# A list-scheduled attention and recurrence kernel: new latencies in its planner, another chunking of the recurrence, another layout of the output

## The chip, the cores and the metric

The kernel runs on one core of a Trainium2 chip. Its time is the device time of one launch in microseconds (us). The engines are called as in the profile: PE (matmul), ACT (activations), DVE (vector), POOL (GpSimd), and SP, which only issues DMAs.

## The reference

`x` holds 8 batches of 1024 tokens of 128 channels, all fp32. Cut to what matters:

```
# layer 0, per batch; 8 heads; a token is a pair (m of 64, g of 16)
scores = q @ k.T / sqrt(128)
a = softmax(softmax(scores over m) over g)
z1 = LN(a @ v @ wo.T + bo + x);  x = LN(relu(z1 @ w1.T + b1) @ w2.T + b2 + z1)
# layer 1, per batch
B = LN(x);  Wi = B @ W.T
scores[i, j] = sum_d v[d] * tanh(Wi[i, d] + Wi[j, d])
t = x + softmax(scores over j) @ B
# layer 1, recurrence over the 1024 tokens, 8 batches side by side
Wx = batch_norm(LN(t) @ W.T);  y[n] = sigmoid(Wx[n] + y[n-1] @ V.T);  out = t + y
```

The scores of layer 1 are symmetric, so some half million pairs per batch, each with 128 tanh, have to be computed.

## The kernel before, in words

`fast_path` does the work; `general_path` is a second program that runs only if a comparison of the inputs' sizes, made at the start, comes out as 0.

**The planner.** The main part is not written in the order in which it runs. Every piece of work is given to a `Plan` (L409) with its engine or a choice of engines, a weight in us for each, what it reads and writes, a priority (lower goes first) and, where it needs one, a choice of buffers. `Plan.emit` (L455) is a list scheduler. It goes through planned time; among the operations that can start within 0.15 us of the earliest start it takes the one of lowest priority number, and writes it at the end of its engine's instruction queue. An operation counts as ready when each producer is done, plus a latency that depends on the producer's engine: `LATENCY` (L425) if the producer ran on another engine, `AGAIN` (L426) if on the same one. The planned times appear nowhere in the program: only the order that they led to, and the choice of engine and of buffer. On the chip each engine takes its queue in that order, and waits by semaphores.

**Layer 0** (`layer0`, L784). For each head and each pair of query tiles: scores on PE (L851) into one of two PSUM tiles `sc`, an exponential on ACT (L854), sums, reciprocals and a division on DVE (L858, L859, L862), a second exponential for the pair on ACT (L871), sums and reciprocals on DVE (L874, L875), a division on POOL (L885), eight transposes on PE (L765) that DVE copies out into `aT` (L777), the product with the values on PE (L899), and an addition on DVE (L906). Small products and transposes go through two PSUM banks, m0 and m1 (`through_bank`). Of the first batch DVE or ACT may empty the banks.

**Layer 1's attention** (`layer1`, L1090, and `group`, L971). The tanh of a row tile are made in groups of k rows by 4. The planner chooses one of three ways for each group when its first row is placed: ACT adds and takes the tanh row by row (L994); or DVE (L998, one operation for each row, which also writes an accumulator) or POOL (L1004, one operation for k rows) adds, and ACT then takes one wide tanh over the group (L1040). Five buffers `th` hold groups. PE multiplies by v (L1057), four groups of 32 columns side by side. After all rows of a tile come an exponential (L1153), products with `B` (L1186) and the addition to X (L1191), whose result t is stored to DRAM in `parked` (L1205) and, normed and projected, to `parked_wx`. While ACT and PE do batch b's attention, batch b + 1's layer 0 runs beside it.

**The recurrence** (from L1324). The 1024 steps are cut into 64 chunks of 16 tokens that run side by side. All chunks are run twice: 16 steps from zero, which give each chunk the state that its neighbour ends with, and then 16 that are kept. (The state forgets fast enough; the comparison at the start tests what this needs.) A step is done in two halves of 32 chunks by 8 batches, 256 columns: `ident` times `ws` (L1365) and V times the previous `y` (L1367) add up in PSUM, ACT takes the sigmoid (L1369), and in the second round DVE copies `y` into `ys` (L1374). `ws` is the normed input in the order of the steps, made by 16 DVE operations (L1346).

**The output.** For each half of the tokens and each batch, PE transposes four tiles (L1382) into one of two PSUM banks, DVE adds `xr`, which is t read back from `parked` (L1340), into one of three buffers `ot` (L1384), and a DMA stores 256 KB (L1386), issued in turn by ACT and SP. A partition of `ot` holds four tokens that lie 128 apart, so the pieces in DRAM are 512 bytes.

Of the kernel before, what the change touches and what calls it, by code (L numbers as in the profile page):

```python
# [9 lines left out]
F32 = mybir.dt.float32  # L10
AF = mybir.ActivationFunctionType
ALU = mybir.AluOpType
AX = mybir.AxisListType
PSUM = bass.MemoryType.PSUM

P = 128
# [382 lines left out]
class Bank:  # L399


    def __init__(self, *choice):
        self.choice = choice

    def __call__(self):
        return self.tile
# [2 lines left out]
class Plan:  # L409
# [12 lines left out]

    LATENCY = {"PE": 0.12, "ACT": 0.08, "DVE": 0.08, "POOL": 0.15, "SP": 8.0}  # L425
    AGAIN = {"PE": 0.0, "ACT": 0.0, "DVE": 0.04, "POOL": 0.1, "SP": 8.0}  # L426

    def __init__(self):
        self.ops = []
# [25 lines left out]
    def emit(self, slack=0.15, switch=0.1, stay=0.015):  # L455
        ops, by = self.ops, self.by
        after = [[] for _ in ops]
        left = []
        for n, o in enumerate(ops):
            before = o[4] | set(o[7])  # L460
            left.append(len(before))
            for d in before:
                after[d].append(n)
        engines = list(self.LATENCY)
        open_ = {e: [] for e in engines}
        free = dict.fromkeys(engines, 0.0)
        done = [0.0] * len(ops)
        began = [0.0] * len(ops)
        places = [None] * len(ops)
        mode = "full"  # L470
        bank_free = {}
        port_free = 0.0
        never = float("inf")
        self.order = []

        def ready_at(n, e):
            t = max((began[d] for d in ops[n][7]), default=0.0)
            for d in ops[n][4]:
                t = max(t, done[d] + (self.AGAIN if by[d] == e else self.LATENCY).get(by[d], 0.0))
            return t  # L480

        def start_at(n, t, e):
            take = ops[n][5]
            if take:
                t = max(t, min(bank_free.get(c[0], 0.0) for c in take.choice))
            if e == "POOL" or (e == "DVE" and ops[n][8]):
                t = max(t, port_free)
            return max(t, free[e])

        def release(n):  # L490
            where = ops[n][0]
            where = where() if callable(where) else where
            if where is None:
                began[n] = done[n] = ready_at(n, None)
                finish(n)
                return
            places[n] = {p[0]: (*p[1:], 0.0) for p in (where if isinstance(where, list) else [where])}
            for e in places[n]:
                open_[e].append((n, ready_at(n, e)))

        def finish(n):
            for a in after[n]:
                left[a] -= 1
                if left[a] == 0:
                    release(a)

        for n in [n for n, c in enumerate(left) if c == 0]:
            release(n)
        while any(open_.values()):
            first, e = min(  # L510
                (min(start_at(n, t, e) for n, t in open_[e]), i) for i, e in enumerate(engines) if open_[e]
            )
            assert first < never
            e = engines[e]
            n, start = min(
                ((n, s) for n, s in ((n, start_at(n, t, e)) for n, t in open_[e]) if s <= first + slack),
                key=lambda c: (ops[c[0]][2][0] + places[c[0]][e][1] + (stay if e == "PE" and ops[c[0]][3] != mode else 0), c[0]),
            )
            _, fn, _, m, _, take, give, _, port = ops[n]
            if take:  # L520
                take.name, take.tile = min(take.choice, key=lambda c: bank_free.get(c[0], 0.0))
                bank_free[take.name] = never
            cost = places[n][e][0]
            if e == "PE":
                if m != mode:
                    cost += switch
                mode = m
            free[e] = start + (cost if e != "SP" else 0.2)
            if e == "POOL" or (e == "DVE" and port):
                port_free = start + cost  # L530
            began[n], done[n], by[n] = start, start + cost, e
            for q in places[n]:
                open_[q] = [c for c in open_[q] if c[0] != n]
            if give:
                bank_free[give.name] = done[n] + self.LATENCY[e]
            self.order.append((n, e, start, done[n]))
            fn(e)
            finish(n)
# [22 lines left out]
def fast_path(ctx: ExitStack, tc: tile.TileContext, a: dict, fits):  # L561
# [5 lines left out]
    nc = tc.nc  # L567
    NB, N, C = a["x"].shape
    H = a["wqn"].shape[1]
    NT = N // P  # L570
# [1 line left out]
    G = 16  # L572
    M = N // G
    SCALE = 1.0 / math.sqrt(C)
    NCH = 64
    LCH = N // NCH
    NX = 2
    NE = 2
# [3 lines left out]
    dram = ctx.enter_context(tc.tile_pool(name="dram", bufs=1, space=bass.MemoryType.DRAM))  # L582
# [4 lines left out]
    def tile_of(pool, name, shape):  # L587
        return pool.tile(shape, F32, tag=name, name=name)
# [6 lines left out]
    wx = tile_of(keep, "wx", [P, NB, N])  # L595
    parked_wx = [tile_of(dram, f"parked_wx{b}", [P, N]) for b in range(NB - 1)]
    wx_stats = tile_of(keep, "wx_stats", [P, NB, 2, 6])

    parked = [tile_of(dram, f"parked{b}", [P, NT, C]) for b in range(NB)]

    def load(pool, name, shape, eng):
        t = pool.tile(shape, F32, tag=name, name=name + "_sb")
# [50 lines left out]
    vf_sb = load(const, "vf", [P, C], nc.sync)  # L653
# [8 lines left out]
    ident = tile_of(const, "ident", [P, P])  # L662
# [308 lines left out]
    def group(it, at0, r0, k, wiT, all_wi, L1, ROWS, fillers, chain, left, both, first_half):  # L971
# [6 lines left out]
        w = N - i0  # L978
# [17 lines left out]
        def add_row(c, r):  # L996

            nc.vector.tensor_scalar(  # L998
                rows(c)[:, r, :], wiT[:, i0 + begin[c] :], w_i(c, r), 0.0, ALU.add, ALU.add, accum_out=unused
            )  # L1000

        def add_rows(eng, c):
# [10 lines left out]
            "POOL": [  # L1013
                (0.27 + 1.62e-3 * k * (w - begin[c]), lambda c=c: add_rows(nc.gpsimd, c)) for c in range(4)
            ],
            "DVE": [(0.30 + 1.04e-3 * (w - begin[c]), lambda c=c, r=r: add_row(c, r)) for c, r in each]
            if k < 4
            else [(0.15 + 1.04e-3 * k * (w - begin[c]), lambda c=c: add_rows(nc.vector, c)) for c in range(4)],
        }
# [152 lines left out]
    def attention(b, it, X, kX, B, kB, E_at, L1):  # L1172
# [27 lines left out]
        if it % 4 != 3:  # L1200
# [1 line left out]
        qh = it // 4  # L1202
        Xg = X[:, 4 * qh : 4 * qh + 4, :]
        add(
            ("SP", 4.0), lambda _: nc.sync.dma_start(out=parked[b][:, 4 * qh : 4 * qh + 4, :], in_=Xg),  # L1205
            r=[kg], w=[("parked", b, qh)], pri=L1,
        )
        layer_norm(Xg, kg, B2, kB2, 4, L1)
# [125 lines left out]
    nc.vector.tensor_tensor(off, beta_sb, off, ALU.subtract)  # L1334


    ys = rn.tile([P, NB, N], F32, tag="ys", name="ys")
    xr = rn.tile([P, NB, NT, C], F32, tag="xr", name="xr")
    for b in range(NB):
        nc.sync.dma_start(out=xr[:, b], in_=parked[b])  # L1340
    steps = ys.rearrange("p b (c l) -> p c b l", l=LCH)

    ws = rn.tile([P, LCH, NCH, NB], F32, tag="ws", name="ws")
    for l in range(LCH):
        step = wx.rearrange("p b (c l) -> p l c b", l=LCH)[:, l]
        nc.vector.tensor_scalar(ws[:, l], step, sc, off, ALU.mult, ALU.add)  # L1346

    with tc.tile_pool(name="ps_w", bufs=2, space=PSUM) as ps_w, tc.tile_pool(
        name="ps_t", bufs=2, space=PSUM
    ) as ps_t:
        HC = NCH // 2
        prev = [None, None]
        for k in range(2 * LCH):
            l = k % LCH
            early = k < LCH
            for half in range(2):
                c0, c1 = half * HC, (half + 1) * HC  # L1360
                skip = 1 if early and half == 0 else 0
                src = ws[:, l, c0 + skip - early : c1 - early, :]
                acc = ps_w.tile([P, HC, NB], F32, tag=f"acc{half}", name=f"acc{half}")
                to = acc[:, skip:, :]
                nc.tensor.matmul(to, ident, src, start=True, stop=k == 0)  # L1365
                if k:
                    nc.tensor.matmul(to, vf_sb, prev[half][:, skip:, :], start=False, stop=True)  # L1367
                y = rn.tile([P, HC, NB], F32, tag=f"y{half}", name=f"y{half}", bufs=3)
                nc.scalar.activation(y[:, skip:, :], to, AF.Sigmoid)  # L1369
                if k == LCH - 1 and half == 0:  # L1370

                    nc.vector.memset(y[:, 0:1, :], 0.0)
                if not early:
                    nc.vector.tensor_copy(steps[:, c0:c1, :, l], y)  # L1374
                prev[half] = y

        n = 0
        for g in range(NT // 4):
            for b in range(NB):
                pt = ps_t.tile([P, 4, C], F32, tag="yt", name="yt")  # L1380
                for i in range(4):
                    nc.tensor.transpose(pt[:, i, :], ys[:, b, (4 * g + i) * P : (4 * g + i + 1) * P], ident)  # L1382
                ot = rn.tile([P, 4, C], F32, tag="ot", name="ot", bufs=3)
                nc.vector.tensor_tensor(ot, pt, xr[:, b, 4 * g : 4 * g + 4, :], ALU.add)  # L1384
                eng = nc.sync if n % 2 else nc.scalar
                eng.dma_start(  # L1386
                    out=a["out"][b, 4 * g * P : 4 * (g + 1) * P, :].rearrange("(t p) c -> p t c", p=P), in_=ot
                )
                n += 1

# [66 lines left out]
```

## Time and profile before

| what | value |
|---|---|
| three timed runs | 5790.97, 5794.7, 5795.5 us; median 5794.7 |
| the profiled execution's own time | 5790.2 us |
| its span, first to last instruction | 5788.3 us |
| mean granted TensorE clock | 0.970 |
| largest groups on POOL, PE and ACT | L1004 3167.8 us, L1057 2121.8 us, L994 2231.2 us, L1040 2069.4 us |
| main part, about | 0 to 5708 us |
| recurrence | 5709.5 to 5766.6 us |
| output | 5765.8 us to the end |

A line of the profile's groups names the line, the engine, what is written from what, the form and the number of times; then the busy time, the mean of one, and the idle time of the engine just before. A line of the waits names who waited for whom; then us in total, times and the longest. A line of the timeline begins with its start and its duration in us, and ends with the idle time before it and what ended that. A row of the stretches gives the length of the stretch and, for PE, PEld (weight loads), DVE, ACT and POOL, the busy time and the number of instructions.

### The profile page before, as it was taken

How to read it: one execution, taken by the hardware profiler on the slowest of the kernel's cores; microseconds unless marked ns; L12 is line 12 of the kernel's file. 1: busy time of each engine (PE TensorE's matmuls, PEld its weight loads, DVE VectorE, ACT ScalarE, POOL GpSimd, SP SyncE). 2: the span in 40 equal slices, each digit the busy share in tenths (PEclk: the TensorE clock that was granted, in tenths of full speed). 3: DMA queues.
4: the chain of work that ended last, by engine and by line, in shares of the span. 5: the costliest groups of instructions: out<-in, count | busy, mean ns of one | idle time of the engine just before them, and what ended most of it. 6: DMA issues, size and time to landing. Idle time of an engine off the chain costs nothing.

```text
span 5788.3 us, 97417 instructions
## 1 busy us (share of the span) xinstructions
PE 5221.0 (90%) x38885; PEld 2783.0 (48%) x38885; DVE 4697.6 (81%) x7236; ACT 5282.6 (91%) x4978; POOL 4218.7 (73%) x2714
## 2 busy tenths in 40 slices
PE   8899999999889999899998998899998999986567
PEld 6555544555445455454554554444554454443125
DVE  7899766877897788977998788977889678898885
ACT  5489999999999999999998999999998999999993
POOL 2352798788788879798786887788796887863871
PEclk9999999999999999999999999999998999998998
DMA  2000000000000000000000000000000000000001
GB/s 59 1 4 1 1 1 5 7 3 1 1 5 8 1 1 5 5 5 1 1 5 5 5 1 1 5 8 1 1 1 3 6 1 1 1 26 8 1 1 63
DMA packets 27328, 37.79 MB, mean 7 GB/s; under 512 B 2464, under 2 KB 19232, under 8 KB 26864
## 3 DMA queue, kind: packets, MB, share of 16 engines
q1 hardware_dynamic: 21760, 27.99, 1.5%
q8 instruction: 307, 5.03, 0.4%
q10 hardware_dynamic: 4944, 3.16, 0.2%
q14 instruction: 157, 1.29, 0.1%
q0 software_dynamic: 160, 0.33, 0.0%
HBM read 19.41 MB, written 12.06 MB: 5 GB/s over the span
## 4 chain that ended last, share of the span: by engine, by line
PE 52%; DVE 23%; ACT 19%; issue 4%; POOL 2%; DMA 0%; DVEq 0%; ACTq 0%; POOLq 0%; SPq 0%
PE sa L1057 19%; PE m L899 11%; PE sc L851 9%; ACT th L1040 8%; ACT th L994 7%; PE m L765 6%; DVE aT L777 2%; DVE th L1004 2%; DVE th L998 2%; DVE stat_e L874 2%; DVE stat_e L858 2%; ACT wx L871 2%; ACT sc L854 2%; DVE wx L862 2%; DVE X L737 2%
## 5 line engine op out<-in xcount | busy, mean ns | idle before, releaser
L1004 POOL TENSOR_TENSOR th<-wiT 128x1024 f32<-128x1024 f32 (+52 forms) x2124 | 3167.8, 1526 | 405.9 <-PE sa L1057 337.5
L1057 PE MATMUL sa<-th,vpat 128*32 128x512 f32 (+33 forms) x24576 | 2121.8, 470 | 230.9 <-ACT th L1040 219.4
L994 ACT ACTIVATE th<-wiT 128x128 f32<-128x128 f32 (+60 forms) x3092 | 2231.2, 795 | 13.7 <-PE sa L1057 13.5
L1040 ACT ACTIVATE th<-th 128x2490 f32<-128x2490 f32 (+50 forms) x760 | 2069.4, 2745 | 98.9 <-DVE th L998 52.5
L885 POOL TENSOR_TENSOR wx<-wx,stat_e 128x1024 f32<-128x1024 f32 x512 | 992.5, 1959 | 862.2 <-DVE stat_e L875 600.9
L1057 PEld LDWEIGHTS sa<-th,vpat 128*32 128x32 f32 x24576 | 674.8, 112 | 1480.7 <-issue 854.4
L851 PE MATMUL sc<-xT,wx 128*128 128x512 f32 x2048 | 982.2, 604 | 24.8 <-DVE wx L862 23.4
L899 PE MATMUL m<-aT,wx 128*128 128x256 f32 x3584 | 883.1, 394 | 15.1 <-DVE aT L777 13.6
L899 PEld LDWEIGHTS m<-aT,wx 128*128 128x128 f32 x3584 | 668.6, 194 | 269.0 <-issue 112.8
L998 DVE TENSOR_SCALAR_CACHE_REDUCE th<-wiT 128x328 f32<-128x328 f32 (+36 forms) x960 | 681.0, 709 | 83.9 <-PE sa L1057 17.8
L858 DVE TENSOR_REDUCE stat_e<-sc 128x16 f32<-128x1024 f32 x512 | 620.5, 1212 | 154.1 <-ACT sc L854 153.0
L777 DVE COPY aT<-m 128x512 f32<-128x512 f32 x927 | 601.4, 676 | 168.7 <-PE m L765 165.1
L874 DVE TENSOR_REDUCE stat_e<-wx 128x128 f32<-128x2048 f32 x256 | 583.7, 2280 | 129.8 <-ACT wx L871 129.0
L765 PE MATMUL m<-ident,wx 128*128 128x128 f32 x3896 | 573.7, 283 | 80.4 <-DVE aT L777 47.0
L862 DVE TENSOR_TENSOR wx<-sc,stat_e 128x1024 f32<-128x1024 f32 x512 | 623.2, 1218 | 22.9 <-POOL wx L885 0.5
L765 PEld LDWEIGHTS m<-ident,wx 128*128 128x128 f32 x3896 | 432.4, 142 | 378.4 <-issue 175.2
L854 ACT ACTIVATE sc<-sc 128x1024 f32<-128x1024 f32 x512 | 513.4, 1005 | 96.6 <-PE sc L851 83.4
L871 ACT ACTIVATE wx<-wx 128x2048 f32<-128x2048 f32 x256 | 486.8, 1902 | 91.4 <-DVE wx L862 88.2
L851 PEld LDWEIGHTS sc<-xT,wx 128*128 128x128 f32 x2048 | 358.4, 192 | 353.2 <-issue 300.3
L1004 DVE TENSOR_TENSOR th<-wiT 128x1024 f32<-128x1024 f32 (+27 forms) x288 | 361.3, 1302 | 2.0 <-ACT th L994 1.1
L875 DVE RECIPROCAL stat_e<-stat_e 128x128 f32<-128x128 f32 x256 | 244.0, 953 | 8.8
L906 DVE TENSOR_TENSOR zs<-m,zs 128x256 f32<-128x256 f32 x212 | 86.0, 406 | 170.0 <-PE m L899 169.4
(168 smaller groups left out, 3040.6 us busy)
## 6 DMA issues: line engine op xcount, KB each, us to landing
xT<-in_xt_dram SPq DMA_DIRECT2D x8, 512.0 KB, 3.7
th<-in_x_dram SPq DMA_DIRECT2D x8, 512.0 KB, 7.0
parked<-X SPq DMA_DIRECT2D x16, 256.0 KB, 2.0
xr<-parked SPq DMA_DIRECT2D x8, 512.0 KB, 7.0
parked_wx<-bT SPq DMA_DIRECT2D x14, 256.0 KB, 2.0
wx<-parked_wx SPq DMA_DIRECT2D x7, 512.0 KB, 3.3
out_dram<-ot ACTq DMA_DIRECT2D x8, 256.0 KB, 2.4
out_dram<-ot SPq DMA_DIRECT2D x8, 256.0 KB, 2.4
```

The lines of the kernel that those rows point to most:

```text
L765: nc.tensor.transpose(bank[:, i * P : (i + 1) * P], s, ident)
L777: nc.vector.tensor_copy(dst, src)
L851: nc.tensor.matmul(sc[:, cols], u[:, qt * P : (qt + 1) * P], xT[:, cols], start=True, stop=True)
L858: nc.vector.tensor_reduce(r1, sc.rearrange("p (m g) -> p g m", g=G), AX.X, ALU.add)
L862: nc.vector.tensor_tensor(e3, sc3, r1.unsqueeze(1).to_broadcast([P, M, G]), ALU.mult)
L885: nc.gpsimd.tensor_tensor(e3, e3, r2[:, q, :].unsqueeze(2).to_broadcast([P, M, G]), ALU.mult)
L899: nc.tensor.matmul(bank()[:, :256], vp[:, t, :], aT[:, t, :], start=t == 0, stop=t == NT - 1)
L994: nc.scalar.activation(rows(c)[:, r, :], wiT[:, i0 + begin[c] :], AF.Tanh, bias=w_i(c, r))
L998: nc.vector.tensor_scalar(rows(c)[:, r, :], wiT[:, i0 + begin[c] :], w_i(c, r), 0.0, ALU.add, ALU.add, accum_out=unused)
L1004: eng.tensor_tensor(rows(c), wiT[:, i0 + begin[c] :].unsqueeze(1).to_broadcast(shape), w_i(c).unsqueeze(2).to_broadcast(shape), ALU.add,)
L1040: lambda _: nc.scalar.activation(slot()[:, : at[4]], slot()[:, : at[4]], AF.Tanh),
L1057: nc.tensor.matmul(sa[32 * c : 32 * c + 32, s:s1], vpat[:, 31 - r0 - r : 63 - r0 - r], rows(c)[:, r, s - at0 - begin[c] : s1 - at0 - begin ...
```

## The change

Four things are changed together.

- In the planner, `LATENCY` goes from 0.08 to 0.15 us up to 0.4 to 0.6, and `AGAIN` of DVE and POOL doubles or nearly so. The weight of one DVE row (L998) goes from 0.30 us and 1.04 ns per column to 0.21 us and 1.05 ns per column. A `Bank` may carry a choice of its own for an engine (`own`); nothing uses it yet.
- The recurrence has 32 chunks of 32 tokens in place of 64 of 16. The first round runs only the last 16 tokens of each chunk, so there are 16 + 32 steps. The halves are now of batches, 4 each with 32 chunks, 128 columns. The 32 `ws` operations are made in the order of use.
- `ys` is laid out so that a tile that is transposed holds every eighth token. A partition of `ot` then holds four neighbouring tokens, and the pieces in DRAM are 2 KB. The output has four PSUM banks and four `ot`, and its loops are exchanged. `parked` is laid out by token, so its stores (L1205) have pieces of 512 bytes where they had 2 KB; `xr` is read in pieces of 4 KB as before.

```diff
-    LATENCY = {"PE": 0.12, "ACT": 0.08, "DVE": 0.08, "POOL": 0.15, "SP": 8.0}
-    AGAIN = {"PE": 0.0, "ACT": 0.0, "DVE": 0.04, "POOL": 0.1, "SP": 8.0}
+    LATENCY = {"PE": 0.6, "ACT": 0.5, "DVE": 0.4, "POOL": 0.6, "SP": 8.0}
+    AGAIN = {"PE": 0.0, "ACT": 0.0, "DVE": 0.08, "POOL": 0.15, "SP": 8.0}
...
-    NCH = 64
+    NCH = 32
...
-    parked = [tile_of(dram, f"parked{b}", [P, NT, C]) for b in range(NB)]
+    parked = [tile_of(dram, f"parked{b}", [N, C]) for b in range(NB)]
...
-            "DVE": [(0.30 + 1.04e-3 * (w - begin[c]), lambda c=c, r=r: add_row(c, r)) for c, r in each]
+            "DVE": [(0.21 + 1.05e-3 * (w - begin[c]), lambda c=c, r=r: add_row(c, r)) for c, r in each]
...
-            ("SP", 4.0), lambda _: nc.sync.dma_start(out=parked[b][:, 4 * qh : 4 * qh + 4, :], in_=Xg),
+            ("SP", 4.0), lambda _: nc.sync.dma_start(
+                out=parked[b][512 * qh : 512 * qh + 512, :].rearrange("(t p) c -> p t c", p=P), in_=Xg
+            ),
...
+    EARLY = 16
+    HB = NB // 2
+    ws = rn.tile([P, LCH, NB, NCH], F32, tag="ws", name="ws")
+    ys = rn.tile([P, NB, NT, NCH, LCH // NT], F32, tag="ys", name="ys")
+    steps = wx.rearrange("p b (c l) -> p l b c", l=LCH)
+    order = [LCH - EARLY + k for k in range(EARLY)] + list(range(LCH))
+    for l in order[:LCH]:
+        nc.vector.tensor_scalar(ws[:, l], steps[:, l], sc, off, ALU.mult, ALU.add)
     with tc.tile_pool(name="ps_w", bufs=2, space=PSUM) as ps_w, tc.tile_pool(
-        name="ps_t", bufs=2, space=PSUM
+        name="ps_t", bufs=4, space=PSUM
     ) as ps_t:
...
+                acc = ps_w.tile([P, HB, NCH], F32, tag=f"acc{half}", name=f"acc{half}")
+                to = acc[:, :, skip:]
+                nc.tensor.matmul(to, ident, ws[:, l, bs, 0 : NCH - skip], start=True, stop=k == 0)
                 if k:
-                    nc.tensor.matmul(to, vf_sb, prev[half][:, skip:, :], start=False, stop=True)
+                    nc.tensor.matmul(to, vf_sb, prev[half][:, :, skip:], start=False, stop=True)
...
                 if not early:
-                    nc.vector.tensor_copy(steps[:, c0:c1, :, l], y)
+                    nc.vector.tensor_copy(ys[:, bs, l % NT, :, l // NT], y)
...
-                ot = rn.tile([P, 4, C], F32, tag="ot", name="ot", bufs=3)
+                ot = rn.tile([P, 4, C], F32, tag="ot", name="ot", bufs=4)
...
-                    out=a["out"][b, 4 * g * P : 4 * (g + 1) * P, :].rearrange("(t p) c -> p t c", p=P), in_=ot
+                    out=a["out"][b].rearrange("(p t) c -> p t c", t=NT)[:, 4 * g : 4 * g + 4, :], in_=ot
```

More of the change, by code (lines that the diff above doesn't have):

```diff
@@ L399, with __init__, of @@
 class Bank:
-    def __init__(self, *choice):
+    def __init__(self, *choice, own=None):
         self.choice = choice
+        self.own = own or {}
+    def of(self, engine):
+        return self.own.get(engine, self.choice)
     def __call__(self):
@@ L484, in start_at @@
             if take:
-                t = max(t, min(bank_free.get(c[0], 0.0) for c in take.choice))
+                t = max(t, min(bank_free.get(c[0], 0.0) for c in take.of(e)))
             if e == "POOL" or (e == "DVE" and ops[n][8]):
@@ L520, in emit @@
             if take:
-                take.name, take.tile = min(take.choice, key=lambda c: bank_free.get(c[0], 0.0))
+                take.name, take.tile = min(take.of(e), key=lambda c: bank_free.get(c[0], 0.0))
                 bank_free[take.name] = never
@@ L1334, in fast_path @@
     nc.vector.tensor_tensor(off, beta_sb, off, ALU.subtract)
-    ys = rn.tile([P, NB, N], F32, tag="ys", name="ys")
     xr = rn.tile([P, NB, NT, C], F32, tag="xr", name="xr")
     for b in range(NB):
[L1340 to L1346, printed above, removed]
+        nc.sync.dma_start(out=xr[:, b], in_=parked[b].rearrange("(p t) c -> p t c", t=NT))
@@ L1353, in fast_path @@
     ) as ps_t:
-        HC = NCH // 2
         prev = [None, None]
-        for k in range(2 * LCH):
-            l = k % LCH
-            early = k < LCH
+        for k, l in enumerate(order):
+            early = k < EARLY
+            skip = 1 if early else 0
             for half in range(2):
[L1360 to L1365, printed above, removed]
-                if k:
[L1367 to L1372, printed above, removed]
+                bs = slice(half * HB, (half + 1) * HB)
+                acc = ps_w.tile([P, HB, NCH], F32, tag=f"acc{half}", name=f"acc{half}")
+                to = acc[:, :, skip:]
+                nc.tensor.matmul(to, ident, ws[:, l, bs, 0 : NCH - skip], start=True, stop=k == 0)
+                if k:
+                    nc.tensor.matmul(to, vf_sb, prev[half][:, :, skip:], start=False, stop=True)
+                y = rn.tile([P, HB, NCH], F32, tag=f"y{half}", name=f"y{half}", bufs=3)
+                nc.scalar.activation(y[:, :, skip:], to, AF.Sigmoid)
+                if k == EARLY - 1:
+                    nc.vector.memset(y[:, :, 0:1], 0.0)
@@ L1373, in fast_path @@
                 if not early:
-                    nc.vector.tensor_copy(steps[:, c0:c1, :, l], y)
+                    nc.vector.tensor_copy(ys[:, bs, l % NT, :, l // NT], y)
                 prev[half] = y
         n = 0
-        for g in range(NT // 4):
-            for b in range(NB):
+        for b in range(NB):
+            for g in range(2):
                 pt = ps_t.tile([P, 4, C], F32, tag="yt", name="yt")
                 for i in range(4):
-                    nc.tensor.transpose(pt[:, i, :], ys[:, b, (4 * g + i) * P : (4 * g + i + 1) * P], ident)
-                ot = rn.tile([P, 4, C], F32, tag="ot", name="ot", bufs=3)
+                    t = 4 * g + i
+                    nc.tensor.transpose(pt[:, i, :], ys[:, b, t].rearrange("p c j -> p (c j)"), ident)
+                ot = rn.tile([P, 4, C], F32, tag="ot", name="ot", bufs=4)
```

## The prediction

> **What bounds the kernel now.** I read the granted clock first (one core, 0.970 of full speed), then the page's busy shares, then the engines' busy time in four stretches that I cut by eye from the 40 slices: layer 0 of the first batch alone, the long middle in which every batch's layer 0 runs beside the previous batch's attention, the last batch's attention, and the end (recurrence and output).
>
> ```profile
> PE 5221.0 (90%) x38885; PEld 2783.0 (48%) x38885; DVE 4697.6 (81%) x7236; ACT 5282.6 (91%) x4978; POOL 4218.7 (73%) x2714
> ```
>
> ```profile
> core 0: us, PE busy (x) PEld busy (x) DVE busy (x) ACT busy (x) POOL busy (x), PEclk, DMA share, GB/s
> 0.00:435.00 435.00, 387.00 (x1843) 258.56 (x1847) 363.58 (x473) 269.34 (x430) 161.77 (x99) 0.98 0.08 21
> 435.00:5075.00 4640.00, 4339.76 (x32875) 2291.30 (x32867) 3768.19 (x5573) 4418.83 (x4038) 3668.38 (x2353) 0.98 0.01 3
> 5075.00:5680.00 605.00, 408.77 (x3758) 162.25 (x3759) 516.26 (x1075) 568.82 (x449) 386.00 (x260) 0.91 0.03 8
> 5680.00:5788.30 108.30, 85.43 (x414) 70.92 (x414) 49.54 (x115) 25.62 (x65) 2.58 (x3) 0.88 0.25 84
> ```
>
> The reader is to see two engines nearly full at once. In the middle PE idles 4640 - 4339.8 = 300 us and ACT 4640 - 4418.8 = 221 us; in the third stretch ACT alone is full (36 us idle); the first belongs to PE. So apart from the end only idle time of PE and ACT can be won, some 220 us at most unless work is removed. What ends that idle time, from the waits of the middle stretch, PE's and then ACT's:
>
> ```profile
> PE m L765 <- DVE aT L777: 103.1, 73, 8.3
> PE sa L1057 <- ACT th L1040: 53.2, 55, 3.9
> PE sc L851 <- DVE wx L862: 21.4, 18, 3.3
> ```
>
> ```profile
> ACT wx L871 <- DVE wx L862: 81.8, 45, 14.4
> ACT sc L854 <- PE sc L851: 36.7, 45, 5.3
> ACT th L1040 <- DVE th L1004: 34.7, 20, 4.0
> ```
>
> These are many waits of about 1 us (us in total, times, longest) of a reader that stands in its engine's queue too close behind its producer. The hop from an end to a reader's start is itself short; after ACT's exponential (ends 5677.77) DVE starts 0.03 us later:
>
> ```profile
> 5677.07 0.70 ACT L1153 ACTIVATE E<-sa 128x640 f32<-128x640 f32 x1 [2.07 <-PE sa L1057]
> 5677.80 0.29 DVE L1159 TENSOR_TENSOR E<-E,half 128x128 f32<-128x128 f32 x1 [4.82 <-ACT E L1153]
> ```
>
> So LATENCY as it is (0.08 to 0.15) tells the hop about rightly, and the waits come from the real times straying from the planned ones, against which 0.1 us is no margin.
>
> **What the skill says.** "TensorE: Matmul & The Clock Gate", Part 1, engine queue depths: ACT, DVE and GpSimd take their queues strictly in order and PE moves only weight loads ahead. The waits above agree: a blocked head holds its engine. "VectorE: DVE Perf Modes", the section on two Vector instructions with no wait between them: an operation that also writes out its accumulator is two instructions. The trace shows the second one:
>
> ```profile
> 5597.39 0.88 DVE L998 TENSOR_SCALAR_CACHE_REDUCE th<-wiT 128x644 f32<-128x644 f32 x1
> 5598.20 0.08 DVE L998 DVE_READ_ACCUMULATOR th<-wiT 128x1 f32 x1
> 5598.41 0.88 DVE L998 TENSOR_SCALAR_CACHE_REDUCE th<-wiT 128x643 f32<-128x643 f32 x1
> ```
>
> One row of 644 takes 1.02 us from start to start. The weight of before says 0.30 + 0.67 = 0.97, the new one 0.21 + 0.68 = 0.89: it is 0.13 us too low. At a width of 303 the rows at 3005.32 and 3005.89 are 0.57 us apart; old 0.62, new 0.53. The new DVE weight is thus the less true one. Two more places are used with their prices below.
>
> **The change, part by part**
>
> 1. *Order of the main program.* Nearly every row of PE, DVE and ACT moves. Counting both programs' instructions: POOL additions at L1004 2124 to 2088, DVE rows at L998 960 to 1092, ACT's single rows at L994 3092 to 3044 and its wide tanh at L1040 760 to 766; PE's work is the same. ACT's elements do not change, so it saves 48 - 6 = 42 fixed parts of about 0.2 us (the planner's 0.18 to 0.2; four rows of 552 at 2999.46 take 2.67 us, 0.67 each, of which the elements are 0.46): 8 us. DVE gains 132 rows of 0.6 to 0.7 us, about 85 us, and goes from 81% to about 83%.
>
> What the larger latency does to the waits I judge from the two orders alone. For each operation with a producer on another engine I add the weights of what stands in the reader's queue between the producer's place in the program and the reader. The reader is short if this is less than the producer's weight plus 0.1 us. Over the middle three quarters of the work PE's short readers fall from 718 to 517 (of some 3060), ACT's from 473 to 342 (of 1680), DVE's from 1168 to 771 (of 2580): 28% fewer on PE and ACT. I scale the measured idle time by that (my choice; there is no row for it): ACT 221 x 0.28 = 62 us, PE 300 x 0.28 = 84 us. Time passes only as fast as the slower of the two is relieved, so 62. Check from the other side: the margin grows by about 0.4 us per hop, and ACT's middle waits are some 210, so up to 84 us could go. Bounds: 0, and 110 (half of ACT's idle time).
>
> Against it stands the DVE weight. 1092 rows planned 0.04 to 0.13 us too short, 0.09 in the mean, are 98 us that DVE runs later than planned, about 1 us in a group of 12 narrow rows, more than the margin of 0.4. DVE idles 872 us in the middle, so most of it is caught up before a reader minds. I pass on a fifth, 20 us; bounds 0 and 98. With the 8 us of rows: 62 + 8 - 20 = 50 us less.
>
> 2. *First stretch.* Short PE readers of the first eighth fall from 153 to 115, a quarter; PE idles 48 us there, of which 10 is one long wait: 0.25 x 38, about 8 us less (0 to 12).
>
> 3. *Third stretch.* ACT is 94% busy with tanh that no other engine can do. Short ACT readers go from 57 to 47, and most of its waits are on DVE rows (20.9 us), which will be later, not earlier. I take 0 (-10 to +10).
>
> 4. *Recurrence.* Before, 32 steps of two halves of 256 columns:
>
> ```profile
> 5740.74 0.38 ACT L1369 ACTIVATE y<-acc 128x256 f32<-128x256 f32 x1 [0.48 <-PE acc L1367]
> 5741.60 0.38 ACT L1369 ACTIVATE y<-acc 128x256 f32<-128x256 f32 x1 [0.48 <-PE acc L1367]
> ```
>
> A half takes 0.86 us, PE's two matmuls of two passes each without a gap (0.215 a pass). From the first sigmoid at 5712.05 to the last one's end at 5766.15 it is 54.1 us. After, 16 + 32 = 48 steps of two halves of 128 columns. A pass of 129 columns with its own weight load costs 0.118 us (12 loads at L1186 in 1.42 us from 5688.81), so eight passes are 0.94 us; by columns alone 0.86. The chain of one half must fit in: weight load to reader's start 0.53 (L1186, 5694.67 to 5695.20); sigmoid 0.29, by "ScalarE: Activation LUTs", What ACT_TABLE_LOAD costs: 186 ns + 0.833 N for immediates (an estimate; at 256 it gives 0.40, the trace 0.38); hop back 0.05: 0.87. So PE still sets the pace: 48 x 0.94 = 45.1 us, 9.0 less. If the chain does (up to 1.08), 52: 2 less; by columns alone 13 less. The first `ws` and the first matmul are half as long, which starts it some 0.7 us sooner. Cover: 32 `ws` operations of about 0.42 us (0.69 for 512 columns less 256 x 1.04 ns) end near 5722, ahead of the first `ys` copy at step 16, near 5726; the 64 copies of some 0.29 us fit in halves of 0.47.
>
> 5. *Output.* Before, three `ot` buffers: every third addition waits until a store lands:
>
> ```profile
> 5769.72 0.69 DVE L1384 TENSOR_TENSOR ot<-yt,xr 128x512 f32<-128x512 f32 x1 [1.10 <-DMA out_dram<-ot]
> 5772.99 0.69 DVE L1384 TENSOR_TENSOR ot<-yt,xr 128x512 f32<-128x512 f32 x1 [0.78 <-DMA out_dram<-ot]
> ```
>
> 3.27 us for three; the first to the last addition take 5782.62 - 5766.49 = 16.1 us. A fourth buffer and pieces of 2 KB: the page's stores of 256 KB land in 2.4 us from `ot` (512 B pieces) and in 2.0 us from `X` (2 KB pieces). A round of four is then the larger of 0.69 + 2.0 + 0.17 = 2.9 and four additions at 0.74, 3.0. "DMA: Bandwidth & Descriptors", Why small descriptors are slow, gives 3 cycles per packet beside its beats of 32 B: 19 for 512 B, 67 for 2 KB, an estimate of 12% less engine time, the same direction. 256 KB in 0.74 us is 354 GB/s, more than this trace shows for stores, so I take 0.78: 15 x 0.78 = 11.7, and 0.4 for the last landing: 4.8 us less (1 to 6).
>
> 6. *Parked rows.* The stores at L1205 go from 2 KB to 512 B pieces. They stand alone on SP's queue, the last is issued at 5697.6, and its reader at 5705.12 leaves 7.5 us for 2.4: nothing. Without that cover it would be 0.4 us.
>
> Sum: -50 - 8 - 0 - 9.7 - 4.8 = -72.5 us from the profiled execution's own 5790.2 us (span 5788.3 and 1.9 around it): 5718. The median of the timed runs, 5794.7, is 4.5 us above that execution; I forecast 5718 without adding this.
>
> **The rivals.**
> - *Margin heals long waits too:* a late engine recovers sooner, and half of ACT's middle idle time goes. 110 + 8 + 8 + 14.5 = 140: 5650. For it: most waits exceed 0.4 us. Against: the short readers fall only by 28%.
> - *Only the end gains:* waits move elsewhere, and two full engines leave no room. 5790 - 14.5: 5776.
> - *Slower: DVE falls behind.* Place: ACT's wide tanh at L1040 behind DVE rows, and PE's transposes behind the copies at L777 that queue after a row group. Price: 98 us of unplanned row time. It decides from the point where a group's 1 us outlasts the margin with no DVE idle time following: if the margin then gains nothing, the passed share must exceed 14.5 / 98 = 15%. With half passed on: 5790 - 14.5 + 49 = 5825. For it: DVE is 91% busy in slices such as 2900 to 3045. Against: 81% in the mean.
>
> That the order does not change is excluded by the count.
>
> **How the numbers follow.** Forecast 0.53, long waits 0.17, end only 0.17, slower 0.13. A difference of 0.2%, 11.6 us, is about what this kernel's measurement can tell from none. Below 5779 lie the first two and some 0.10 of the third: faster 0.80, same 0.07, slower 0.13. The range goes from the 5650 of the long waits to 5790, which leaves the slower case and half of the lowest out; the forecast's own bounds are 5690 to 5750.
>
> **What would show it.** ACT's idle time in the middle near 160 us and PE's near 220; ACT's waits on L862 and L851 shorter; DVE rows 132 more, its busy time near 4780; first to last sigmoid near 45 us with PE gapless; additions of the output 0.74 to 0.8 us apart with no wait on a store. Wrong would be: the middle no shorter, ACT's wait on L998 or L1004 well above 66 us, or sigmoids of one half more than 1.0 us apart.

## The result, and the profile after

The changed kernel takes 5697.5 us (median of four runs, 5696.8 to 5699.6) against 5792.8 us (5790.7 to 5795.5): a ratio of 0.9837, 95% interval 0.9825 to 0.9849, 95 us less. The forecast was 5718, 72 us less than the profiled execution of before. The profiled execution of the changed kernel took 5699.6 us, with a span of 5697.8. Line numbers are 5 higher than before in the main part and mostly 7 or 8 higher at the end.

The page's first line of the changed kernel:

```profile
PE 5166.6 (91%) x39013; PEld 2765.7 (49%) x39013; DVE 4754.1 (83%) x7545; ACT 5263.0 (92%) x4964; POOL 4186.4 (73%) x2678
```

To compare the two traces I cut both at the same events: the first product with v (L1057, now L1062), the last scores (L851, now L856), and the last exponential of layer 1 (L1153, now L1158). The busy time by stretch, before and then after (length, then PE, PEld, DVE, ACT and POOL):

```profile
0.00:327.50 327.50, 279.90 (x1251) 194.85 (x1251) 263.33 (x331) 174.00 (x304) 107.75 (x69) 0.98 0.10 26
327.50:5197.50 4870.00, 4554.15 (x34165) 2409.63 (x34168) 3978.72 (x5926) 4623.67 (x4262) 3807.32 (x2434) 0.98 0.01 4
5197.50:5677.80 480.30, 299.87 (x3055) 106.44 (x3053) 404.80 (x863) 459.32 (x349) 301.06 (x209) 0.91 0.02 5
5677.80:5788.30 110.50, 87.03 (x419) 72.13 (x419) 50.72 (x118) 25.62 (x65) 2.58 (x3) 0.87 0.25 82
```

```profile
0.00:306.00 306.00, 273.96 (x1239) 190.53 (x1239) 256.33 (x344) 166.33 (x298) 102.24 (x66) 0.99 0.10 28
306.00:5102.00 4796.00, 4493.93 (x34008) 2389.39 (x34008) 4004.82 (x6083) 4589.50 (x4195) 3762.28 (x2390) 0.98 0.01 3
5102.00:5602.10 500.10, 324.17 (x3222) 118.16 (x3220) 435.00 (x952) 479.49 (x376) 319.29 (x221) 0.91 0.03 8
5602.10:5697.80 95.70, 74.50 (x547) 67.63 (x547) 57.99 (x167) 27.72 (x97) 2.58 (x3) 0.84 0.26 95
```

The first stretch is 21.5 us shorter, the middle 74.0, the end 14.8; the third is 19.8 longer, because 20 us of ACT's work and 24 of PE's now lie there instead of in the middle. Middle and third together give 54.2 us. On ACT's side these are 40 us of idle time (246 to 206 in the middle) and 14 of busy time. On PE's side idle time falls by only 18 us (14 of them in the middle, 316 to 302), and busy time by 36, with the same work.

ACT's waits in the middle stretch so cut, before and then after:

```profile
ACT wx L871 <- DVE wx L862: 83.4, 47, 14.4
ACT sc L854 <- PE sc L851: 44.7, 49, 5.3
ACT th L1040 <- DVE th L998: 38.2, 20, 4.7
```

```profile
ACT wx L876 <- DVE wx L867: 75.4, 26, 11.4
ACT sc L859 <- PE sc L856: 37.5, 32, 7.5
ACT th L999 <- DVE wiT L1109: 21.1, 5, 15.6
ACT th L1045 <- DVE th L1003: 13.2, 12, 2.8
```

The reader is to see fewer waits and longer ones. The three rows of before fall from 116 to 70 waits, many of the short ones being gone; a wait for `wiT`, 5 times and up to 15.6 us, is new.

The recurrence after, two sigmoids of one and the next half and PE's matmul that the second waits for:

```profile
5664.12 0.28 ACT L1376 ACTIVATE y<-acc 128x128 f32<-128x128 f32 x1 [0.17 <-PE acc L1374]
5664.14 0.39 PE L1374 MATMUL acc<-y,vf_sb 128*128 128x128 f32 x2
5664.57 0.28 ACT L1376 ACTIVATE y<-acc 128x128 f32<-128x128 f32 x1 [0.17 <-PE acc L1374]
```

The timeline has a sigmoid every 0.45 us, one for each half, so a step takes 0.90. First sigmoid to the end of the last: 5635.89 to 5680.48, 44.6 us (54.1 before). The output's additions after:

```profile
5680.65 2.47 DVE L1392 TENSOR_TENSOR ot<-yt,xr 128x512 f32<-128x512 f32 x4
5683.62 2.68 DVE L1392 TENSOR_TENSOR ot<-yt,xr 128x512 f32<-128x512 f32 x4 [0.49 <-DMA out_dram<-ot]
5686.55 2.73 DVE L1392 TENSOR_TENSOR ot<-yt,xr 128x512 f32<-128x512 f32 x4 [0.25 <-DMA out_dram<-ot]
```

Rounds of four take about 2.93 us and still end on a store, but with waits of 0.25 to 0.5 us; first to last addition take 11.3 us (16.1 before).

### The profile page after: what moved, and what is told of

It reads as the page before. It is cut to its first block, busy times and chain, and to the rows that moved or that the text cites. A ratio compares the mean times of both kernels' runs of the same rounds, so it can differ in the third digit from the quotient of the medians.

```text
span 5697.8 us, 97791 instructions
## 1 busy us (share of the span) xinstructions
PE 5166.6 (91%) x39013; PEld 2765.7 (49%) x39013; DVE 4754.1 (83%) x7545; ACT 5263.0 (92%) x4964; POOL 4186.4 (73%) x2678
## 4 chain that ended last, share of the span: by engine, by line
PE 40%; DVE 24%; ACT 23%; issue 4%; POOL 1%; DMA 0%; DVEq 0%; ACTq 0%; POOLq 0%
PE sa L1062 16%; ACT th L1045 10%; ACT th L999 9%; PE m L904 8%; PE sc L856 6%; PE m L770 4%; DVE th L1003 3%; DVE stat_e L879 3%; DVE th L1009 3%; DVE stat_e L863 2%; DVE aT L782 2%; ACT wx L876 2%; DVE wx L867 2%; ACT sc L859 2%; PE m L1191 1%
## 5 line engine op out<-in xcount | busy, mean ns | idle before, releaser
L1009 POOL TENSOR_TENSOR th<-wiT 128x896 f32<-128x896 f32 (+55 forms) x2088 | 3131.7, 1535 | 436.8 <-PE sa L1062 400.4
L1062 PE MATMUL sa<-th,vpat 128*32 128x512 f32 (+27 forms) x24576 | 2104.4, 466 | 223.6 <-ACT th L1045 212.6
L999 ACT ACTIVATE th<-wiT 128x516 f32<-128x516 f32 (+55 forms) x3044 | 2203.1, 798 | 37.1 <-DVE wiT L1109 21.1
L1045 ACT ACTIVATE th<-th 128x4096 f32<-128x4096 f32 (+54 forms) x766 | 2083.8, 2746 | 49.0 <-DVE th L1003 28.0
L1062 PEld LDWEIGHTS sa<-th,vpat 128*32 128x32 f32 x24576 | 674.8, 111 | 1470.4 <-issue 834.4
L856 PE MATMUL sc<-xT,wx 128*128 128x512 f32 x2048 | 985.7, 606 | 36.0 <-DVE wx L867 35.8
L904 PE MATMUL m<-aT,wx 128*128 128x256 f32 x3584 | 862.2, 389 | 14.7 <-DVE aT L782 12.0
L1003 DVE TENSOR_SCALAR_CACHE_REDUCE th<-wiT 128x384 f32<-128x384 f32 (+47 forms) x1092 | 758.1, 694 | 86.3 <-PE sa L1062 15.0
L856 PEld LDWEIGHTS sc<-xT,wx 128*128 128x128 f32 x2048 | 357.3, 192 | 367.1 <-issue 301.7
L1009 DVE TENSOR_TENSOR th<-wiT 128x1024 f32<-128x1024 f32 (+28 forms) x280 | 392.1, 1439 | 3.9 <-PE sa L1062 3.0
L738 POOL TENSOR_TENSOR stat<-stat,neg_half 128x4 f32<-128x4 f32 x64 | 65.3, 1020 | 245.4 <-DVE stat L735 230.6
```

What stands on the lines that cost most here:

```text
L856: nc.tensor.matmul(sc[:, cols], u[:, qt * P : (qt + 1) * P], xT[:, cols], start=True, stop=True)
L904: nc.tensor.matmul(bank()[:, :256], vp[:, t, :], aT[:, t, :], start=t == 0, stop=t == NT - 1)
L999: nc.scalar.activation(rows(c)[:, r, :], wiT[:, i0 + begin[c] :], AF.Tanh, bias=w_i(c, r))
L1003: nc.vector.tensor_scalar(rows(c)[:, r, :], wiT[:, i0 + begin[c] :], w_i(c, r), 0.0, ALU.add, ALU.add, accum_out=unused)
L1009: eng.tensor_tensor(rows(c), wiT[:, i0 + begin[c] :].unsqueeze(1).to_broadcast(shape), w_i(c).unsqueeze(2).to_broadcast(shape), ALU.add,)
L1045: lambda _: nc.scalar.activation(slot()[:, : at[4]], slot()[:, : at[4]], AF.Tanh),
```

## The experiments

The prediction left open whether the margin or the new weight of a DVE row made the main part shorter, and whether one order of a list schedule says anything about its planner at all. Three theories went into the runs: the margin; the weight, which moves rows to DVE; and luck, that any disturbance moves the order and the time by tens of us.

**The end alone.** LATENCY, AGAIN and the weight as before; the rest as changed.

> The changed kernel with LATENCY, AGAIN and the DVE weight of before: only the recurrence in 32 chunks and the output are new. All theories expect the main part as before and 15 us less at the end: 5778 us. If the order of the main part also depends on the end, it would show as another time at which the last wx_stats stands; none expects that.

Measured 5776.0 us against 5792.1, ratio 0.9970 (0.9958 to 0.9982): 16 us less. Its last stretch is 94.8 us (110.5 before), its middle 4873.7, as before:

```profile
328.20:5201.90 4873.70, 4557.73 (x34165) 2408.07 (x34168) 3981.66 (x5926) 4623.84 (x4261) 3808.08 (x2434) 0.98 0.01 4
```

So the end is worth what was forecast, and an order that is repeated repeats its time within 4 us of 4870.

**The margin alone, and with the old weight.** The first changes only these two lines in the kernel before; the second has it too, and the new end, but not the new weight.

```diff
-    LATENCY = {"PE": 0.12, "ACT": 0.08, "DVE": 0.08, "POOL": 0.15, "SP": 8.0}
-    AGAIN = {"PE": 0.0, "ACT": 0.0, "DVE": 0.04, "POOL": 0.1, "SP": 8.0}
+    LATENCY = {"PE": 0.6, "ACT": 0.5, "DVE": 0.4, "POOL": 0.6, "SP": 8.0}
+    AGAIN = {"PE": 0.0, "ACT": 0.0, "DVE": 0.08, "POOL": 0.15, "SP": 8.0}
```

> The kernel before with the new LATENCY and AGAIN alone. Theory of the margin (half a microsecond between producer and reader removes waits): 70 to 80 us less, 5713 to 5723. Theory of the weight (the cheaper DVE row moves rows off ACT, and that is the gain): within 15 us of before, 5780 to 5793. Theory of luck (any disturbance of a list schedule moves the time by tens of us either way): anything from 5700 to 5830.

> The changed kernel with the old weight of a DVE row, 0.30 us and 1.04 ns. Margin: the weight that is truer gives 0 to 20 us, so 5677 to 5697. Weight: the gain of the main part goes, near 5770. Luck: anything from 5640 to 5770.

Measured 5745.3 us (0.9917, 0.9904 to 0.9931) and 5732.2 us (0.9894, 0.9879 to 0.9910). Both have one order of the main part (middle 4841.7 and 4842.8 us) and differ by the end, 13 us. The margin alone gives 47 us: less than its theory said, far more than the weight's theory allowed. With the new end and the old weight the time is above what the margin's theory forecast and below what the weight's did; only luck's wide range holds it.

**The weight alone.**

```diff
-            "DVE": [(0.30 + 1.04e-3 * (w - begin[c]), lambda c=c, r=r: add_row(c, r)) for c, r in each]
+            "DVE": [(0.21 + 1.05e-3 * (w - begin[c]), lambda c=c, r=r: add_row(c, r)) for c, r in each]
```

> The kernel before with the new weight of a DVE row alone. Margin: DVE runs later than planned with no margin, 0 to 30 us slower, 5793 to 5823. Weight: most of the 76 us, near 5725. Luck: anything from 5700 to 5830.

Measured 5811.4 us (1.0034, 1.0022 to 1.0046), 19 us slower. Taken singly this looks as if the weight cost 19 us without a margin and gained 35 with it (5732.2 to 5697.5). That the next runs did not bear out.

**Disturbances of the weight within the margin.** The changed kernel with 0.20 and with 0.22 in place of 0.21, and with the weight that the trace of before shows, 0.25 + 1.17e-3.

> The changed kernel with 0.20 us in place of 0.21 us as the fixed part of a DVE row, a disturbance of 1 to 2% of that weight. If the 33 us that the weight gave within the margin are its doing: within 5 us of 5697. If any such disturbance reshuffles the order and moves the time by tens of us: more than 10 us away.

> The changed kernel with 0.22 us in place of 0.21 us, the disturbance on the other side of the one that gave 5754. A draw around the mean of the margin's runs (5697, 5754, 5720, 5732, 5730 with the end taken off): 5700 to 5755. If the changed kernel's 5697 belongs to its weight: within 10 us of 5697.

> The changed kernel with a DVE row weighed as the rows stand apart in the trace of before, 0.25 us and 1.17 ns per column (0.57 measured and 0.60 so at 303; 1.02 and 1.00 at 644). If what counts with a margin is that the plan is true: under 5697. If it is that the weight is low, so that rows go to DVE: at or above the old weight's 5732.

Measured 5754.1 us (0.9930, 0.9917 to 0.9944), 5729.8 (0.9895, 0.9880 to 0.9910) and 5720.4 (0.9873, 0.9858 to 0.9888). A change of 0.01 us in a weight of some 0.4 to 1.3 us made the kernel 57 us slower one way and 32 the other. So the 35 us (33 in the expectation) were not the weight's doing. The weight taken from the trace lies between its two forecasts and bears out neither. The kernel with 0.20, middle and third stretch:

```profile
306.00:5150.70 4844.70, 4514.12 (x33899) 2394.12 (x33898) 3973.87 (x6050) 4576.77 (x4195) 3771.15 (x2406) 0.98 0.01 3
5150.70:5658.40 507.70, 335.02 (x3330) 126.71 (x3329) 444.14 (x979) 489.80 (x352) 325.43 (x225) 0.92 0.03 8
```

Its first stretch is the same 306 us, its middle 49 us longer than the changed kernel's: 61 us more of ACT idle time there and 13 less busy.

**A disturbance without the margin.** The kernel before with 0.31 in place of 0.30.

> The kernel before with 0.31 us in place of 0.30 us as the fixed part of a DVE row: a disturbance without a margin, so far too small to matter by itself. If an order of the main part is a draw with a spread of 20 us or so around a mean that the margin sets: 5770 to 5815, the mean of before and of the new weight alone being 5802. If orders without a margin are as likely to fall near 5740 as those with one, then the margin is not the cause: below 5765.

Measured 5809.5 us (1.0029, 1.0018 to 1.0040), 18 us slower, by an edit that says nothing about the machine, and in the other direction than the new weight's.

**The size of the margin.** The changed kernel with all four values of LATENCY at nine tenths, three quarters, about half, and doubled; AGAIN as changed.

```diff
-    LATENCY = {"PE": 0.6, "ACT": 0.5, "DVE": 0.4, "POOL": 0.6, "SP": 8.0}
+    LATENCY = {"PE": 1.2, "ACT": 1.0, "DVE": 0.8, "POOL": 1.2, "SP": 8.0}
```

> The changed kernel with LATENCY at nine tenths (0.54, 0.45, 0.36, 0.54). A draw: 5700 to 5755. It is also a try at a faster order: under 5697 would beat both kernels, which one draw in five or six should.

> The changed kernel with LATENCY at three quarters (0.45, 0.375, 0.3, 0.45). A draw with a mean that is hardly above that of the full margin: 5700 to 5760; under 5697 would beat both kernels.

> The changed kernel with LATENCY about halfway between old and new (0.35, 0.3, 0.25, 0.37). Margin as the cause: between end alone plus weight (5811 - 16 = 5795) and the changed kernel (5697), near 5745. Luck: no order with the dose, anything from 5680 to 5800.

> The changed kernel with LATENCY doubled (1.2, 1.0, 0.8, 1.2). Margin: half of the middle's waits are longer than 0.5 us, so another 10 to 30 us less, 5667 to 5690, unless the planner now sees engines idle that are not, which would show as a longer first or third stretch. Luck: 5680 to 5800.

Measured 5734.5 us (0.9903, 0.9888 to 0.9918), 5750.2 (0.9923, 0.9910 to 0.9937), 5734.9 (0.9899, 0.9884 to 0.9914) and 5909.1 (1.0199, 1.0185 to 1.0213). Half a margin does about as well as a whole one; none beat the changed kernel. Doubled, it is slower by 2%, a clear miss of the margin's theory. (Its exception, a longer first or third stretch, is met by the first, but most of the loss lies in the middle.) Its middle stretch and ACT's waits in it:

```profile
336.70:5345.80 5009.10, 4583.91 (x34161) 2444.36 (x34160) 4025.42 (x6321) 4610.11 (x4194) 3669.75 (x2340) 0.97 0.01 3
```

```profile
ACT sc L859 <- PE sc L856: 163.3, 44, 46.3
ACT wx L876 <- DVE wx L867: 90.1, 22, 43.7
```

The waits are as few as in the changed kernel, but up to 46 us long. They are no hops any more: the order lets ACT come to a layer 0 operation long before PE has the scores. The first stretch is longer too, 336.7 us. A likely reason is that layer 0's long chain takes longer in a plan with large latencies, and is paced wrongly against the tanh; this is argued from the waits and was not tried.

**Taken together.** All on the new end (16.1 us taken off where the end was old), one entry for each order of the main part:

| planner | times, us | mean |
|---|---|---|
| LATENCY as before | 5776.0, 5795.3, 5793.4 | 5788 |
| half | 5734.9 | |
| three quarters | 5750.2 | |
| nine tenths and whole | 5697.5, 5754.1, 5729.8, 5720.4, 5732.2, 5734.5 | 5728 |
| doubled | 5909.1 | |

Within the last but one row the standard deviation is 19 us, far more than a repeated order shows. The margin is worth 5788 - 5728 = 60 us, with a 95% interval of 32 to 88 if the orders are taken as independent draws; no order with a margin of half to whole is as slow as the fastest one without. The low weights (0.20 to 0.22: 5697.5, 5754.1, 5729.8, 5734.5, mean 5729) and the truer ones (5720.4, 5732.2, mean 5726) do not differ. The changed kernel is the fastest of six draws, 31 us below their mean, and before is the fastest of its three, by 12. So the 95 us are 60 of the margin, 16 of the end, and 19 of draws.

Where the margin acts is the same in the six orders with nine tenths or the whole of it: the first stretch takes 303 to 308 us (328 or 329 without a margin), the middle 4832 to 4845, the changed kernel's 4796 apart (4870 to 4878 without). The third is 480 to 508 us (480 to 492 without). In the mean the first stretch gains 23 us, the middle 44, and the third loses 5.

How it acts shows when ACT's idle time in the middle stretch of every trace is split by the length of the single wait:

| planner | in waits under 4 us, us | in longer waits, us | first stretch, us |
|---|---|---|---|
| LATENCY as before, three orders | 196 (186 to 208) | 65 (53 to 77) | 328 or 329 |
| half | 159 | 71 | 334 |
| three quarters | 125 | 140 | 305 |
| nine tenths and whole, six orders | 127 (107 to 142) | 110 (99 to 126) | 303 to 308 |
| doubled | 132 | 267 | 337 |

A margin removes a third of the short waits and makes long ones longer or more frequent. Beyond three quarters no more short waits go, and doubled the long ones more than eat up the gain. What makes the long ones was not tried. `AGAIN`, raised by 0.04 us for DVE and 0.05 for POOL in every run with a margin, was never tried alone: the steps from half to doubled show that LATENCY matters, not that `AGAIN` does nothing.

## Why the prediction was right, and where it was off

- *Order of the main program, middle and third stretch: forecast -50, measured -54.* The mechanism was right: fewer readers stand close behind their producers, and the short waits go. ACT's idle time in waits under 4 us fell by 86 us in the middle, from 193 to 107, and by 69 in the mean of the orders (forecast 62). What the working lacks is that a margin also makes long waits: those of 4 us and more rose by 46 us, from 53 to 99, and by 45 in the mean. The 20 us that it takes off for late DVE rows stood in their place by accident, and so ACT's idle time came out at -40 where the sum has -42. ACT's busy time fell by 14 (forecast 8). The agreement to a few us is luck in a second way too: in the mean of the orders the two stretches gain 39 us, and with a spread of 19 us from order to order a count of short readers can give that mean and no single order. The range held it because it was wide for other reasons.
- *PE's 84 us of idle time: wrong.* They fell by 14, and by 18 with the third stretch. By the prediction's own rule, that time passes only as fast as the slower of the two is relieved, 18 us was then all that could be gained. The other 36 are PE's busy time, which fell with the same work, and part of that is the clock:

```profile
core 0: 5788.3 us, clock 0.970
```

```profile
core 0: 5697.8 us, clock 0.975
```

  The share not granted is 0.030 x 5788 = 174 us before and 0.025 x 5698 = 142 after, so at most 31 us of the 54 by which PE's busy time fell in all (PE also idles in some of that time); 12.5 are the end's. In the middle and third stretch alone the share not granted fell by 29 us, from 154 to 126. The rest was not resolved. I had read the clock and left it out of the working.
- *First stretch: forecast -8, measured -21.5.* The term was mis-sized: I set aside one long wait of 10 us as out of a margin's reach, and it is gone in the changed kernel; the other PE waits there fell by 6 us, and PE's busy time by 6, of which some 2 are the half clock that followed that wait (last section; 4.4 us of PE's work lie in it). This is no draw: in all six orders with nine tenths or the whole margin the stretch takes 303 to 308 us. As the first stretch of before has it:

```profile
PE sa L765 <- DVE X L926: 10.0, 1, 10.0
```

- *DVE weight: a fifth of 98 us passed on, 20 us.* No run shows this cost. The true weight is no better than the low one by more than the spread (5726 and 5729). DVE did get its 132 rows (busy 4697.6 to 4754.1 us; forecast 4780), and ACT's waits on these rows fell from 38 to 13 us in the middle where I had feared more. The slower rival has nothing for it: the disturbance to the other side, 0.31, was as slow as the low weight.
- *Long waits too, 5650:* no; apart from the one of the first stretch the long ones grew in sum (ACT's of 4 us and more from 53 to 99 us in the middle; one for `wiT` is 15.6). *Only the end, 5776:* no.
- *Recurrence: forecast 45.1 us, measured 44.6.* A pass of 128 columns takes 0.112 us (weight loads 0.45 us apart for four passes), eight 0.90, where the working had 0.94. Passes that need the last y start 0.11 us after the pass before them, as those do that don't, and PE has no gap, so PE sets the pace, as forecast. The chain of a half is close behind: a weight load starts at 5664.48, 0.08 us after the end of the sigmoid at 5664.12 whose y it reads. At 0.90 a step 48 steps are 43.2 us; the rest is a start at half clock, in which the sigmoids come 0.85 us apart. The 44.6 us are thus two small misses that cancel. The two rows are the start and what follows; the third figure from the end is the granted clock:

```profile
5635.90:5640.70 4.80, 4.49 (x21) 4.49 (x22) 4.80 (x12) 1.80 (x7) 0.00 (x0) 0.50 1.02 400
5640.70:5680.50 39.80, 39.80 (x358) 39.80 (x358) 24.36 (x80) 24.62 (x89) 0.00 (x0) 1.00 0.05 18
```

  The sigmoid took 0.28 us; "ScalarE: Activation LUTs", What ACT_TABLE_LOAD costs, gave an estimate of 0.29.
- *Output: forecast 11.7 us, measured 11.3.* The stores of 2 KB pieces land in 2.1 to 2.2 us (2.4 before), not 2.0. That no addition would wait for a store was wrong, with no effect on the sum. The stores at L1205 went from 2.0 to 2.3 us, and nothing waits for them.

## What to carry to other kernels

Half a microsecond of planned latency, some five times what was planned before, made this list schedule some 1% faster in the mean of its orders; twice that made it 2% slower. It does so by trading short waits for long ones, so count both. The likely reason, that real times stray from the planned ones, was not tried. But one order is a draw: a change of 0.01 us in one weight moved the time by 57 us, so before a planner's parameter is credited with a gain, run several orders that differ by edits which should not matter, with and without it. In a step-by-step recurrence, count PE's passes for a step against the chain of one half; fewer columns pay only until the two meet.

## What the runs showed of the hardware

PE's busy time is no measure of its work: a pass costs about twice as much while the clock is halved. In the first stretch of the kernel before, PE waits 10 us for DVE; then two matmuls of the same form, at half clock and 3.5 us later at full clock:

```profile
240.26 1.08 PE L765 MATMUL sa<-ident,X 128*128 128x128 f32 x4 [10.02 <-DVE X L926]
242.04 2.07 PE L939 MATMUL sa<-zs,w_sb 128*128 128x512 f32 x2 [0.69 <-ACT zs L775]
245.53 1.02 PE L939 MATMUL sa<-zs,w_sb 128*128 128x512 f32 x2
```

The ends of matmuls are modelled in the profile; the sigmoids of the recurrence after, 0.85 us apart at half clock and then 0.45, show nearly the same without them.

"TensorE: Matmul & The Clock Gate", Part 1, says that the clock falls to half after an idle window of some 3.4 us and comes back with sustained work. The stretches at half clock in these traces do last multiples of 3.4 us. But PE need not idle for all of such a window, nor in one piece. In these two rows PE idles 2.1 of the first 3.4 us, in pieces of 0.8 us at most, and the next window runs at half clock (the third figure from the end is the granted clock):

```profile
1576.60:1580.00 3.40, 1.31 (x8) 0.84 (x8) 3.11 (x8) 2.33 (x1) 3.40 (x4) 1.00 0.00 0
1580.00:1583.40 3.40, 2.92 (x20) 0.99 (x24) 3.40 (x4) 3.40 (x4) 3.40 (x4) 0.51 0.02 5
```

With the whole trace of before cut into such windows, 53 of the 54 windows at full clock in which PE idled 2 us or more are followed by half clock, and one of the 1488 with less than 1.6 us; after the change it is 35 of 35 and none of 1490. In between both happen. Full clock came back only after a window with less than 0.6 us of idle time (66 returns before, 45 after). So in this case it is about 2 us of idle time within 3.4 that halve the clock.

The mean granted clock agrees in direction: 0.960 with waits of up to 46 us (doubled margin), 0.970 before, 0.975 after. So a schedule in which PE's gaps bunch less gains a second time (66 falls to half clock before, 46 after). How much of the spread between orders comes this way was not separated: the kernel with 0.20 has 0.971, nine tenths has 0.976 with a time near the mean, and 0.31, slower than before, has 0.973.
